# Two 256 x 256 transposes per graph moved from TensorE to VectorE, in 32 x 32 blocks

## The chip, the cores and the metric

The kernel runs on one core of a Trainium2 chip. A core has five engines that work side by side, each with a queue of instructions that it executes in order: TensorE (PE in the profile: matrix products; PEld its weight loads), VectorE (DVE), ScalarE (ACT), GpSimd (POOL) and SyncE (SP, which only issues transfers here). Sixteen DMA engines move data between the chip's memory (HBM) and the on-chip buffers (SBUF). Engines wait for each other by semaphores. The metric is the device time of one execution in microseconds, the median of several runs.

## The reference

64 graphs of 256 nodes with 256 features go through two layers; each layer adds its result to its input and normalises over the features.

```python
# layer 0
deg = adj.sum(-1);  d = deg ** -0.5                    # deg 0 counts as 1
x1 = layernorm(x + (d[:, :, None] * adj * d[:, None, :] + alpha * I) @ x @ W.T + b)
# layer 1, on x1; xc is x1 transposed to (features, nodes)
h = relu(bn1(conv1(xc)))                               # 1 tap
x_conv = relu(bn2(conv2(h)) + xc).T                    # 17 taps along the nodes
s = x1 @ w_se.T + b_se                                 # 3 coordinates per node
A = exp(-squared_distance(s, s)) * adj
x_nmp = A @ relu(x1 @ w_msg.T + b_msg)
r, z, n = gates([x_conv, x_nmp], x1)                   # a GRU cell
out = layernorm(x1 + (1 - z) * n + z * x1)
```

Inputs and weights are float32. Everything is computed in float32.

## The kernel before

A matmul on TensorE sums over the partition axis of both operands, so what is to be summed must lie on the partitions. Two operands lie the wrong way round: adj, whose transpose `adjT` (256 x 256, two halves of 128 partitions) feeds layer 0's product and the mask of the distances, and `x1`, the output of layer 0, whose transpose fills the first half of the tile `xn` and feeds conv1 and the messages. Both are transposed on TensorE today.

**Stages.** The graphs go in four groups of 16. Conv2 with its 17 taps is done in the frequency domain: the node axis is cut in pieces of 32, DFT'd (`p_dft`, L469), multiplied per frequency with the transformed weights (`p_k`, L526, over a whole group) and turned back; VectorE does the turning. So each group has three kinds of work: the front of its 16 graphs (layer 0 and layer 1 up to the message passing), the products, and the gates of its graphs (`p_rz` L804, `p_n` L841). Beside the front of the first 13 graphs, the transformed conv2 weights are made: taps are loaded (L276 to L278, SP), scaled (L285, DVE), transformed (`p_u`, L293, eight matmuls), copied out of TensorE's banks (L296, ACT, four copies into `u_set`), combined (difference L298 on DVE, sum L299 on POOL) and stored (L301). In the second group a few graphs' fronts run among the products and the others alone; in the later groups they run among the products or beside the gates of the group before.

**Layer 0 of a graph** (`layer0`, L337), in three pieces. The first: degrees by ScalarE with an accumulated sum (L347), `dis` = deg to the power −1/2 on POOL (L360), four transposes of 128 x 128 on TensorE into the bank `p_adjT` (L369) and one ScalarE copy into `adjT` (L370), the scaled diagonal on DVE (L372), x scaled by `dis` into the tile `x1` (L382, ACT; noted as `X_SCALED`), and x + b (L383, POOL). The second: `p_hT` (L390) and its copy (L395). The third: `p_out` (L400), scaled and added to x by DVE into `x1` (L405), the layer norm of `x1` in place (statistics on DVE L311 to L313, the power on POOL L314, L322 on DVE, the last step on ACT L324), and a store of `x1` to `x1_d` in HBM (L410, on ScalarE's DMA queue), which the gates read later.

**Layer 1 of a graph** (`layer1`, L422), in seven pieces: x1 transposed if it isn't yet (L419, copy L420); conv1 (`p_conv` L434, added bias L437 on DVE, relu L438 on ACT); messages (`p_msg` L455, L458, L459); the DFT (L469, copies L474); the coordinates as rows (L482 to L486); the distances (L493), exp (L494) and the product with `adjT` (L495); the message passing (`p_nmp` L502, copied to the second half of `xn` at L506, stored at L507). Where the graph is in the set `ALONE`, the transposes of x1 of the next graph are issued just before `p_nmp` (L498).

**What sets the order.** The program is a set of generators. `graphs` (L917) runs layer 1 of graph g; between its pieces it puts the pieces of layer 0 of graph g+2 and "other" work, by the table

```python
PLACES = (("other",), ("layer0",), (), (), ("layer0",), ("other", "layer0"), ())
```

A framework schedules what the generators issue, tracks the tiles, inserts the waits, and leaves a fixed order for each engine. A tile of a pool with `bufs=n` rotates over n buffers; who writes it waits for the last reader of the buffer's old contents. `adj_t`, `x_t`, `x1` and `xn` have two buffers, `h`, `hT` and `msg` one. `load(g)` (L95) issues adj and x of graph g whole, 256 KB each, on SP's queue.

The output of conv2 is transposed too (`transposed`, L765, bank `p_xcT` L772, with relu on ScalarE), which the change leaves as it is.

Of the kernel before, what the change touches and what calls it, by code (L numbers as in the profile page):

```python
# [9 lines left out]
F32 = mybir.dt.float32  # L10
# [4 lines left out]
P = 128  # L15
# [11 lines left out]
def kernel(  # L27
# [27 lines left out]
    nc = tc.nc  # L55
    B, N, D = x.shape
# [3 lines left out]
    NCH = N // P  # L60
    DCH = D // P


    FL, NT = 48, 32
    GT = N // NT
    Q = P // GT
    NQ = B // Q
    assert N == 256 and D == 256 and B % Q == 0 and TAPS == FL - NT + 1 and FL == 3 * NT // 2
# [6 lines left out]
    loads = ctx.enter_context(tc.tile_pool(name="loads", bufs=2))  # L75
# [4 lines left out]
    def bank(name):  # L80
        return ps.tile([P, 512], F32, tag="bank", name=name)
# [10 lines left out]

    xin, ain = {}, {}

    def load(g):  # L95
        if g >= B:
            return
        ain[g] = loads.tile([P, NCH, N], F32, name="adj_t")
        nc.sync.dma_start(ain[g], adj[g].rearrange("(c p) m -> p c m", p=P))
        xin[g] = loads.tile([P, NCH, D], F32, name="x_t")  # L100
        nc.sync.dma_start(xin[g], x[g].rearrange("(c p) f -> p c f", p=P))

# [9 lines left out]
    vectors = const.tile([16, P], F32, name="bn_in")  # L112
    neg_half = const.tile([P, 4], F32)
    nc.vector.memset(neg_half, -0.5)
    load(0)
    nc.scalar.dma_start(alpha_t, bcast_rows(alpha, 1))

    nc.scalar.copy(bc1[:, :4], neg_half)
    for i, a in enumerate((bn1_g, bn2_g, bn1_b, bn2_b, bn1_m, bn2_m, bn1_v, bn2_v)):
        (nc.sync if i % 2 else nc.scalar).dma_start(vectors[2 * i : 2 * i + 2], a.rearrange("(c p) -> c p", p=P))  # L120
    nc.scalar.dma_start(w0, w0T.rearrange("(k p) o -> p k o", p=P))
    load(1)
    nc.sync.dma_start(b0_t, bcast_rows(b0, D))
    nc.sync.dma_start(wc1[:, :, :D], conv1T.rearrange("(k p) o -> p k o", p=P))
    nc.sync.dma_start(wc1[:, :, D:], w_seT.rearrange("(k p) o -> p k o", p=P))
# [204 lines left out]
    x1_d = [dram.tile([Q, N, D], F32, name=f"x1_d{q}") for q in range(NQ)]  # L330
    xn_d = [dram.tile([P, 2 * DCH, N], F32, name=f"xn_d{g}") for g in range(B)]
    XN = {}
    ALONE = set()
    ADJT, X1, X_SCALED, DIAGONAL = {}, {}, {}, {}


    def layer0(g):  # L337

        a_t, x_t = ain.pop(g), xin.pop(g)

        adjT = work.tile([P, NCH, 3, P], F32, name="adjT", bufs=3)
        ADJT[g] = adjT

        deg = small.tile([P, NCH], F32, name="deg")
        def degrees():
            for c in range(NCH):
                nc.scalar.activation(  # L347
                    adjT[:, c, 0:2, :].rearrange("p n q -> p (n q)"), a_t[:, c, :], AF.Copy,
                    accum_out=deg[:, c : c + 1],
                )  # L350

        if g == 1:

            with tc.issue_after(X_SCALED[0]):
                degrees()
        else:
            degrees()
        nc.vector.scalar_tensor_tensor(deg, deg, 0.0, deg, op0=ALU.is_equal, op1=ALU.add)  # L358
        dis = small.tile([P, NCH], F32, name="dis")
        nc.gpsimd.tensor_tensor(dis, deg, neg_half[:, :NCH], op=ALU.pow)  # L360
        adeg = small.tile([P, NCH], F32, name="adeg")
        nc.vector.tensor_scalar(adeg, deg, alpha_t, None, op0=ALU.mult)

        p = bank("p_adjT").rearrange("p (c n) -> p c n", c=NCH)
        for mc in range(NCH):
            for c in range(NCH):
                nc.tensor.transpose(p[:, mc, c * P : (c + 1) * P], a_t[:, c, mc * P : (mc + 1) * P], ident)  # L369
        copied = nc.scalar.copy(adjT[:, :, 0:3:2, :], p.rearrange("p c (n q) -> p c n q", q=P))  # L370
        for mc in range(NCH):
            DIAGONAL[g] = nc.vector.scalar_tensor_tensor(  # L372
                adjT[:, mc, 1, :], ident, adeg[:, mc : mc + 1], adjT[:, mc, 2 * mc, :],
                op0=ALU.mult, op1=ALU.add,
            ).ins


        x1 = work.tile([P, NCH, D], F32, name="x1")
        X1[g] = x1
        with tc.issue_after(copied.ins) if g < 2 else ExitStack():  # L380
            for c in range(NCH):
                X_SCALED[g] = nc.scalar.activation(x1[:, c, :], x_t[:, c, :], AF.Copy, scale=dis[:, c : c + 1]).ins  # L382
        nc.gpsimd.tensor_tensor(x_t, x_t, b0_t.unsqueeze(1).to_broadcast([P, NCH, D]), op=ALU.add)  # L383

        yield
        hT = work.tile([P, DCH, N], F32, name="hT", bufs=1)
        p = bank("p_hT").rearrange("p (k n) -> p k n", k=DCH)
        for k in range(DCH):
            for mc in range(NCH):
                nc.tensor.matmul(  # L390
                    p[:, k, :], x1[:, mc, k * P : (k + 1) * P],
                    adjT[:, mc, 1 - mc : 3 - mc, :].rearrange("p n q -> p (n q)"),
                    start=mc == 0, stop=mc == NCH - 1,
                )
        nc.scalar.copy(hT, p)  # L395
        yield
        p = bank("p_out0").rearrange("p (c o) -> p c o", c=NCH)
        for c in range(NCH):
            for k in range(DCH):
                nc.tensor.matmul(  # L400
                    p[:, c, :], hT[:, k, c * P : (c + 1) * P], w0[:, k, :], start=k == 0, stop=k == DCH - 1
                )
        for c in range(NCH):
            mark(
                nc.vector.scalar_tensor_tensor(  # L405
                    x1[:, c, :], p[:, c, :], dis[:, c : c + 1], x_t[:, c, :], op0=ALU.mult, op1=ALU.add
                )
            )
        layernorm(x1, nc.scalar)
        nc.scalar.dma_start(x1_d[g // Q][g % Q].rearrange("(c p) d -> p c d", p=P), x1)  # L410
        yield

    def x1_transposed(g):
        x1 = X1.pop(g)
        xn = XN[g] = work.tile([P, 2 * DCH, N], F32, name="xn")
        p = bank("p_x1T").rearrange("p (k n) -> p k n", k=DCH)
        for k in range(DCH):
            for c in range(NCH):
                nc.tensor.transpose(p[:, k, c * P : (c + 1) * P], x1[:, c, k * P : (k + 1) * P], ident)  # L419
        nc.scalar.copy(xn[:, :DCH], p)  # L420

    def layer1(g, V, place):  # L422
# [34 lines left out]
                )  # L457
        mark(nc.vector.tensor_tensor(msg, p, bmsg_t.unsqueeze(1).to_broadcast([P, NCH, D]), op=ALU.add))  # L458
        nc.scalar.activation(msg, msg, AF.Relu)  # L459
        yield  # L460


# [31 lines left out]
            nc.scalar.activation(aT[:, c].rearrange("p n q -> p (n q)"), p, AF.Exp, bias=nsq[:, c : c + 1], scale=2.0)  # L494
        mark(nc.vector.tensor_mul(aT, aT, adjT[:, :, 0:3:2, :]))  # L495
        yield
        if g in ALONE:
            x1_transposed(g + 1)  # L498
        p = bank("p_nmp").rearrange("p (k n) -> p k n", k=DCH)
        for k in range(DCH):  # L500
# [416 lines left out]
    def graphs(first, part, V, others):  # L917


        for i in part:  # L920
            load(first + i + 3)
            given = {"layer0": layer0(first + i + 2) if first + i + 2 < B else iter(()), "other": others[i]}
            for piece, _ in enumerate(layer1(first + i, V, i)):
                yield
                for name in PLACES[piece]:
                    if next(given[name], "end") != "end":
                        yield
            yield from given["other"]

    with tc.tile_pool(name="setup", bufs=1) as setup:  # L930
# [2 lines left out]
        nc.sync.dma_start(bmsg_t, bcast_rows(b_msg, D))  # L933
        firsts = merge(layer0(0), layer0(1))
        run(take(firsts, 2))
        load(2)
        tables(setup)
        run(firsts)
        scale2 = next(batch_norms(setup))
# [65 lines left out]
    for q in range(NQ):  # L1005
        first = (q + 1) * Q
        more = q + 1 < NQ
        end = complex_end(q)
        if more:
            if q:  # L1010
                others = [take(late, 3 if i % 3 == 0 else 2) for i in range(AHEAD)]
            else:
                others = [nothing() for _ in range(AHEAD)]
                ALONE.update(range(first, first + AHEAD))
            begin = graphs(first, range(AHEAD), V2, others)
        sums(0)
        real = real_transform()
        for step in range(STEPS):
            if step < 4:
                run(products(step))  # L1020
            else:
                run(merge(products(step), take(real, 1)))
                run(complex_begin(step))
            if q:
                run(take(late, (0, 1, 1, 1, 1, 1, 2, 1, 2, 1, 2, 1)[step] if more else step % 2))
            else:
                run(take(begin, 3))
        run(real)
        if not q:
            run(paced(begin, end, RATES[q]))  # L1030
        elif more:
            run(paced(chain(merge(take(late, 20), take(begin, 6), 3), begin), end, RATES[q]))
        else:
            run(paced(late, end, RATES[q]))
            run(end)
        if more:
            run(late)
            run(end)
            for f in range(0, FL, 12):
                nc.scalar.copy(V[:, f : f + 12, :, : AHEAD * GT], V2[:, f : f + 12])  # L1040
            if q == 0:
                scope.close()
                gate = ctx.enter_context(tc.tile_pool(name="gate", bufs=2))
            early = gates(q, range(EARLY))
            others = [take(early, 5 if q == 0 else 2) for _ in range(Q)]
            run(graphs(first, range(AHEAD, Q), V, others))
            run(early)
            if q == 0:
                scope, AHEAD, V2 = open_ahead(6)
                ctx.enter_context(scope)  # L1050
            late = gates(q, range(EARLY, Q))
        else:
            run(gates(q, range(Q)))
# [53 lines left out]
```

## Time and profile before

| | before |
|---|---|
| time, median of 3 runs | 2166.91 us (2165.66 to 2167.95) |
| span of the profiled execution | 2165.1 us |
| TensorE clock granted | 0.99 to 1.00 of full speed |
| DMA | 305.65 MB in 251,182 packets, mean 141 GB/s |
| L370, copy of `p_adjT` by ScalarE | 64 of 576 ns, 36.9 us busy |
| L495, product with `adjT` by VectorE | 64 of 692 ns, 44.3 us busy |
| chain that ended last | TensorE has 20% of the span, POOL 3%, VectorE 2% |

The page of a profile first gives the busy time of each engine with its share of the span, then the span in 40 equal slices, where each digit is the busy share of a slice in tenths (9 is 90% or more); for the DMA row it is the mean over the 16 engines. In the table of groups, a row is one line of the program on one engine: output <- inputs, partitions x elements, the count, then busy microseconds and mean nanoseconds of one, then the idle time of the engine just ahead of them and what ended it. In the timeline, a row is start in microseconds, length, engine, line, operation, tiles, count and, in brackets, the idle time before it. Engines are pipelined: the distance between the starts of neighbours says what an instruction costs, its length how long it is in flight.

### The profile page before, as it was taken

Reading aid. Unit: us, or ns where it says so; the run is one execution under the profiler, and the core shown is the slowest. Engines: PE = TensorE matmul, PEld = TensorE weight load, DVE = VectorE, ACT = ScalarE, POOL = GpSimd, SP = SyncE. Lnnn points to the kernel's source line nnn. Section 1 sums busy time; section 2 is a strip of 40 time slices with the busy share of each in tenths; the row PEclk is TensorE's granted clock in tenths of the full one; section 3 lists DMA queues with packets and bytes.
Section 4 is the critical chain, followed back from the end, with each engine's and each line's share of the span. In section 5 each row is a group of like instructions: output and inputs, shape, how many; then the busy total and the mean of one; then the engine's idle time right before and its main releaser. Section 6 shows DMA issues by size and latency. Waiting matters only on the chain. (4 is left out here: it accounts for less than half of the span.)

```text
span 2165.1 us, 29037 instructions
## 1 busy us (share of the span) xinstructions
PE 2063.7 (95%) x9805; PEld 1749.6 (81%) x9805; DVE 1546.6 (71%) x3691; ACT 833.8 (39%) x1847; POOL 665.5 (31%) x640
## 2 busy tenths in 40 slices
PE   7999999888999999999999999899999998999998
PEld 5788788776778887788888888778888887888887
DVE  5555568775568798865556989775556889977776
ACT  4565643456331133455443122446443112222222
POOL 2444310122431243323222133323231124444442
PEclk9999999999999999999999999999999999999999
DMA  4765656435346644343336654334334844444441
GB/s 125 224 198 183 212 185 208 148 132 154 90 132 214 201 116 122 97 132 112 106 95 189 203 162 122 113 103 137 97 98 132 246 114 122 126 122 103 113 106 55
DMA packets 251182, 305.65 MB, mean 141 GB/s; under 512 B 18174, under 2 KB 229714, under 8 KB 251034
## 3 DMA queue, kind: packets, MB, share of 16 engines
q1 hardware_dynamic: 183530, 200.46, 30.1%
q10 hardware_dynamic: 44480, 67.39, 8.8%
q0 software_dynamic: 23024, 35.95, 8.6%
q8 instruction: 78, 1.28, 0.2%
q14 instruction: 70, 0.57, 0.1%
HBM read 200.62 MB, written 103.06 MB: 140 GB/s over the span
## 5 line engine op out<-in xcount | busy, mean ns | idle before, releaser
L841 PE MATMUL p_n<-wn,inputs 128*128 128x256 f32 x1536 | 357.6, 387 | 9.9 <-DVE first L817 9.4
L804 PE MATMUL p_rz<-wrz,sums 128*128 128x256 f32 x1536 | 348.8, 380 | 3.9 <-POOL sums L783 3.1
L841 PEld LDWEIGHTS p_n<-wn,inputs 128*128 128x128 f32 x1536 | 290.4, 193 | 57.3 <-DVE first L817 13.1
L804 PEld LDWEIGHTS p_rz<-wrz,sums 128*128 128x128 f32 x1536 | 289.7, 190 | 47.8 <-issue 5.2
L804 PE MATMUL p_rz<-wrz,inputs 128*128 128x256 f32 x1152 | 271.6, 379 | 0.0
L314 POOL TENSOR_TENSOR ln_rs<-ln_rs,neg_half 128x2 f32<-128x2 f32 x129 | 101.2, 784 | 521.4 <-DVE ln_rs L313 410.2
L804 PEld LDWEIGHTS p_rz<-wrz,inputs 128*128 128x128 f32 x1152 | 217.5, 190 | 29.7 <-ACT inputs L774 0.4
L853 ACT ACTIVATE nn<-gn 128x256 f32<-128x256 f32 x128 | 53.2, 416 | 333.1 <-DVE gn L850 333.0
L526 PE MATMUL p_k<-u,VM 128*128 128x256 f32 x736 | 174.3, 380 | 0.3 <-DMA u<-ud 0.3
L360 POOL TENSOR_TENSOR dis<-deg,neg_half 128x2 f32<-128x2 f32 x64 | 46.6, 727 | 408.9 <-DVE deg L358 405.5
L783 POOL TENSOR_TENSOR sums<-inputs 128x384 f32<-128x384 f32 x64 | 67.8, 1059 | 332.9 <-ACT inputs L774 326.2
L324 ACT ACTIVATE x_g<-x_g,ln_mr,ln_rs 128x256 f32<-128x256 f32 x128 | 70.0, 593 | 245.3 <-DVE ln_mr L322 245.3
L526 PEld LDWEIGHTS p_k<-u,VM 128*128 128x128 f32 x736 | 138.5, 190 | 20.8 <-DMA u<-ud 1.2
L469 PE MATMUL p_dft<-fwd,h 128*128 128x240 f32 x512 | 120.2, 379 | 20.7 <-ACT h L438 19.7
L390 PE MATMUL p_hT<-adjT,x 128*128 128x256 f32 x512 | 126.7, 390 | 12.8 <-DVE adjT L372 7.7
L434 PE MATMUL p_conv<-wc,xn 128*128 128x259 f32 x512 | 126.2, 388 | 6.8 <-ACT xn L420 5.6
L383 POOL TENSOR_TENSOR x_t<-x_t,b_t 128x512 f32<-128x512 f32 x64 | 87.6, 1370 | 138.9 <-ACT x L382 88.1
L469 PEld LDWEIGHTS p_dft<-fwd,h 128*128 128x128 f32 x512 | 95.8, 192 | 41.2 <-ACT h L438 34.5
L495 DVE TENSOR_TENSOR aT<-aT,adjT 128x512 f32<-128x512 f32 x64 | 44.3, 692 | 114.6 <-ACT aT L494 114.6
L400 PE MATMUL p_out<-w,hT 128*128 128x256 f32 x512 | 124.4, 386 | 1.5 <-ACT hT L395 0.9
L455 PE MATMUL p_msg<-wmsg,xn 128*128 128x256 f32 x512 | 121.3, 380 | 0.0
L502 PE MATMUL p_nmp<-aT,msg 128*128 128x256 f32 x512 | 121.1, 379 | 0.2 <-DVE aT L495 0.2
(154 smaller groups left out, 3897.9 us busy)
## 6 DMA issues: line engine op xcount, KB each, us to landing
u<-ud SPq DMA_DIRECT2D x284, 256.0 KB
xn_d<-xn ACTq DMA_DIRECT2D x64, 512.0 KB
inputs<-xn_d SPq DMA_DIRECT2D x64, 512.0 KB
ud<-u_set POOLq DMA_DIRECT2D x39, 480.0 KB, 6.1
adj_t<-in_adj_dram SPq DMA_DIRECT2D x64, 256.0 KB
x_t<-in_x_dram SPq DMA_DIRECT2D x64, 256.0 KB
x_d<-x ACTq DMA_DIRECT2D x64, 256.0 KB
xc_d<-VM SPq DMA_DIRECT2D x64, 256.0 KB
```

Of the source, the lines that this page charges most:

```text
L314: nc.gpsimd.tensor_tensor(rs[:, : len(chunks)], rs[:, : len(chunks)], neg_half[:, : len(chunks)], op=ALU.pow)
L324: nc.scalar.activation(y[:, c, :], y[:, c, :], AF.Identity, bias=mr[:, c : c + 1], scale=rs[:, c : c + 1])
L383: nc.gpsimd.tensor_tensor(x_t, x_t, b0_t.unsqueeze(1).to_broadcast([P, NCH, D]), op=ALU.add)
L390: nc.tensor.matmul(p[:, k, :], x1[:, mc, k * P : (k + 1) * P], adjT[:, mc, 1 - mc : 3 - mc, :].rearrange("p n q -> p (n q)"), start=mc == ...
L400: nc.tensor.matmul(p[:, c, :], hT[:, k, c * P : (c + 1) * P], w0[:, k, :], start=k == 0, stop=k == DCH - 1)
L434: nc.tensor.matmul(p, x1T[:, k, c * P : (c + 1) * P], wc1[:, k, :], start=k == 0, stop=k == DCH - 1)
L455: nc.tensor.matmul(p[:, c, :], x1T[:, k, c * P : (c + 1) * P], wmsg[:, k, :], start=k == 0, stop=k == DCH - 1)
L469: nc.tensor.matmul(p[:, t0 * FL : t1 * FL], h[:, c, k * P : (k + 1) * P], fwd[:, first : first + t1 - t0, :].rearrange("p t f -> p (t f)") ...
L502: nc.tensor.matmul(p[:, k, :], msg[:, mc, k * P : (k + 1) * P], aT[:, mc].rearrange("p n q -> p (n q)"), start=mc == 0, stop=mc == NCH - 1,)
L526: nc.tensor.matmul(p[:, j * D : (j + 1) * D], v[:, k, :], u[:, k, :], start=k == 0, stop=k == DCH - 1)
L804: nc.tensor.matmul(p[:, j * D : (j + 1) * D], a[:, k], wrz[:, b, k], start=k == 0, stop=k == HALF - 1)
L841: nc.tensor.matmul(p[:, o * D : (o + 1) * D], lhsT, w, start=j == 0, stop=j == len(part) - 1)
```

## The change

adj (graphs 2 to 63) and x1 (graphs 1 to 63) are transposed by VectorE. Its transpose works inside 32 x 32 blocks: each block is transposed in its place, the blocks themselves aren't exchanged. So the load exchanges them: block (i, j) is fetched to where block (j, i) was. `fetch_blocks` does it with four transfers for one matrix, each to 32 partitions, with 16 runs of 32 elements (128 bytes) a partition. adj is therefore loaded twice, once as it is for the degrees and once by blocks, in the same two rotating buffers; x1 is read back from its store in HBM, during layer 1 of the graph before it. The tile `x1` then needs to live only until its store is through and gets one buffer instead of two, which makes room for the blocks of x1. The transposes of x1 of the next graph are now issued ahead of `p_nmp` for every graph. The load of adj moves behind layer 0's first piece. The purpose is to take transposes and copies off TensorE and ScalarE.

```diff
+    def fetch_blocks(blocks, y):
+        for b in range(NB):
+            nc.sync.dma_start(
+                blocks[b * RB : (b + 1) * RB], y.rearrange("(s r) (k b j) -> b r k s j", r=RB, k=DCH, j=RB)[b]
+            )
...
+        a_t, a_b = loads.tile([P, NCH, N], F32, name="adj_t", tag="adj"), None
+        nc.sync.dma_start(a_t, adj[g].rearrange("(c p) m -> p c m", p=P))
+        if g > 1:
+            a_b = loads.tile([P, DCH, N // RB, RB], F32, name="adj_blocks", tag="adj")
+            fetch_blocks(a_b, adj[g])
...
-        p = bank("p_adjT").rearrange("p (c n) -> p c n", c=NCH)
-        for mc in range(NCH):
-            for c in range(NCH):
-                nc.tensor.transpose(p[:, mc, c * P : (c + 1) * P], a_t[:, c, mc * P : (mc + 1) * P], ident)
-        copied = nc.scalar.copy(adjT[:, :, 0:3:2, :], p.rearrange("p c (n q) -> p c n q", q=P))
+        if a_b is None:
...
+        else:
+            nc.vector.transpose(
+                adjT[:, :, 0:3:2, :].rearrange("p k n (s r) -> p k n s r", r=RB),
+                a_b.rearrange("p k (n s) j -> p k n s j", n=NCH),
+            )
...
-        x1 = work.tile([P, NCH, D], F32, name="x1")
+        x1 = work.tile([P, NCH, D], F32, name="x1", bufs=1, tag="x1" if g else "x1_blocks")
...
+    def fetched(g):
+        XB[g] = work.tile([P, DCH, N // RB, RB], F32, name="x1_blocks", bufs=1)
+        fetch_blocks(XB[g], x1_d[g // Q][g % Q])
...
         xn = XN[g] = work.tile([P, 2 * DCH, N], F32, name="xn")
+        if g:
+            nc.vector.transpose(xn[:, :DCH].rearrange("p k (s r) -> p k s r", r=RB), XB.pop(g))
+            return
...
         nc.scalar.activation(msg, msg, AF.Relu)
+        if g + 1 < B:
+            fetched(g + 1)
         yield
...
-        if g in ALONE:
+        if g + 1 < B:
             x1_transposed(g + 1)
...
-            load(first + i + 3)
+            load_x(first + i + 3)
...
                     if next(given[name], "end") != "end":
+                        if name == "layer0" and piece == 1:
+                            load_adj(first + i + 3)
                         yield
...
-                ALONE.update(range(first, first + AHEAD))
```

More of the change, by code (lines that the diff above doesn't have):

```diff
@@ L65 @@
     GT = N // NT
+    RB = 32
+    NB = P // RB
     Q = P // GT
@@ L93, with load_adj, load_x @@
     xin, ain = {}, {}
-    def load(g):
+    def fetch_blocks(blocks, y):
[3 more added lines that the diff above has]
+            )
+    def load_adj(g):
         if g >= B:
             return
-        ain[g] = loads.tile([P, NCH, N], F32, name="adj_t")
-        nc.sync.dma_start(ain[g], adj[g].rearrange("(c p) m -> p c m", p=P))
+        a_t, a_b = loads.tile([P, NCH, N], F32, name="adj_t", tag="adj"), None
[3 more added lines that the diff above has]
+            fetch_blocks(a_b, adj[g])
+        ain[g] = a_t, a_b
+    def load_x(g):
+        if g >= B:
+            return
         xin[g] = loads.tile([P, NCH, D], F32, name="x_t")
@@ L114 @@
     nc.vector.memset(neg_half, -0.5)
-    load(0)
+    load_adj(0)
+    load_x(0)
     nc.scalar.dma_start(alpha_t, bcast_rows(alpha, 1))
@@ L121 @@
     nc.scalar.dma_start(w0, w0T.rearrange("(k p) o -> p k o", p=P))
-    load(1)
+    load_adj(1)
+    load_x(1)
     nc.sync.dma_start(b0_t, bcast_rows(b0, D))
@@ L332 @@
     XN = {}
-    ALONE = set()
+    XB = {}
     ADJT, X1, X_SCALED, DIAGONAL = {}, {}, {}, {}
     def layer0(g):
-        a_t, x_t = ain.pop(g), xin.pop(g)
+        a_t, a_b, x_t = *ain.pop(g), xin.pop(g)
         adjT = work.tile([P, NCH, 3, P], F32, name="adjT", bufs=3)
@@ L362, in layer0 @@
         nc.vector.tensor_scalar(adeg, deg, alpha_t, None, op0=ALU.mult)
-        p = bank("p_adjT").rearrange("p (c n) -> p c n", c=NCH)
-        for mc in range(NCH):
-            for c in range(NCH):
-                nc.tensor.transpose(p[:, mc, c * P : (c + 1) * P], a_t[:, c, mc * P : (mc + 1) * P], ident)
-        copied = nc.scalar.copy(adjT[:, :, 0:3:2, :], p.rearrange("p c (n q) -> p c n q", q=P))
+        if a_b is None:
+            p = bank("p_adjT").rearrange("p (c n) -> p c n", c=NCH)
+            for mc in range(NCH):
+                for c in range(NCH):
+                    nc.tensor.transpose(p[:, mc, c * P : (c + 1) * P], a_t[:, c, mc * P : (mc + 1) * P], ident)
+            copied = nc.scalar.copy(adjT[:, :, 0:3:2, :], p.rearrange("p c (n q) -> p c n q", q=P))
+        else:
[3 more added lines that the diff above has]
+            )
         for mc in range(NCH):
@@ L415, in x1_transposed @@
         xn = XN[g] = work.tile([P, 2 * DCH, N], F32, name="xn")
+        if g:
+            nc.vector.transpose(xn[:, :DCH].rearrange("p k (s r) -> p k s r", r=RB), XB.pop(g))
+            return
         p = bank("p_x1T").rearrange("p (k n) -> p k n", k=DCH)
@@ L935 @@
         run(take(firsts, 2))
-        load(2)
+        load_adj(2)
+        load_x(2)
         tables(setup)
```

## The prediction

> **What bounds the kernel now.** I read the busy shares first, then the slices, the costliest groups, and last the timeline of single graphs.
>
> ```profile
> PE 2063.7 (95%) x9805; PEld 1749.6 (81%) x9805; DVE 1546.6 (71%) x3691; ACT 833.8 (39%) x1847; POOL 665.5 (31%) x640
> ...
> PE   7999999888999999999999999899999998999998
> ...
> DVE  5555568775568798865556989775556889977776
> ...
> DMA  4765656435346644343336654334334844444441
> ```
>
> TensorE (PE) is busy 95% of the span, and from slice 2 on in every slice; the trace's own ends of matmuls are modelled, so the weight loads' 81% are the firmer figure. VectorE (DVE) has 29% free on average, but the digits 8 and 9 of its row show stretches that are nearly full. So whatever leaves TensorE is time won, as long as TensorE waits for nothing new. The change touches these groups, kept apart by shape:
>
> ```profile
> L369 PE MATMUL p_adjT<-ident,adj_t 128*128 128x128 f32 x256 | 39.8, 279 | 7.1 <-DMA adj_t<-in_adj_dram 7.1
> ...
> L419 PE MATMUL p_x1T<-ident,x 128*128 128x128 f32 x256 | 39.1, 275 | 0.0
> L420 ACT COPY xn<-p_x1T 128x512 f32<-128x512 f32 x64 | 37.6, 587 | 6.1 <-PE p_x1T L419 5.8
> ```
>
> After the first bar stand busy time and the mean ns of one, after the second the idle time before them. The transposes overlap in the pipeline, so 275 ns isn't what one costs. The timeline of one graph of the first stage (start, length) tells:
>
> ```profile
> 163.84 1.23 DVE L298 TENSOR_TENSOR u_set<-u_set,u_set 120x1024 f32<-120x1024 f32 x1
> ...
> 165.10 0.88 DVE L405 SCALAR_TENSOR_TENSOR x<-p_out,dis,x_t 128x256 f32<-128x256 f32 x2
> ...
> 166.02 0.60 PE L419 MATMUL p_x1T<-ident,x 128*128 128x128 f32 x4
> ...
> 166.45 1.89 PE L293 MATMUL p_u<-taps,dft_w 85*120 85x256 f32 x8
> ...
> 168.18 1.92 PE L434 MATMUL p_conv<-wc,xn 128*128 128x259 f32 x8
> ...
> 169.68 1.09 ACT L324 ACTIVATE x<-x,ln_mr,ln_rs 128x256 f32<-128x256 f32 x2 [2.39 <-DVE ln_mr L322]
> ```
>
> From L419's start to that of the next matmuls is 0.43 us; 169.94 to 170.37 gives the same for L369's four. L469 starts at 156.34 and again at 172.37, so a graph takes 16.03 us here. To be noted for later: conv1 (L434) starts 2.16 us after the x1 transposes, and waits for no part of the layer norm of the next graph (L324), which comes after it.
>
> **What the skill says.** The Trainium skill, "VectorE: DVE Perf Modes", The three transpose paths, gives VectorE's 32x32 blocks 311 ns for 128x128 bf16, inside blocks only, hence the exchanged blocks in the load. No DVE transpose is in this trace. "TensorE: Matmul & The Clock Gate", Part 4, has about 275 ns for a PE transpose in a kernel: the trace agrees with 275 to 279 ns as a duration, but shows a pitch of 0.11. "DMA: Bandwidth & Descriptors", Why small descriptors are slow, states a fixed cost per packet; in this trace 1 KB packets take some 57 ns (queue 1: 30.1% of 16 x 2165.1 us over 183,530 packets).
>
> **The change part by part.**
>
> *Leaves TensorE and ScalarE.* adj of graphs 2 to 63 (62 sets) and x1 of graphs 1 to 63 (63 sets): 125 sets of four transposes x 0.435 = **−54.4 us** of PE, if nothing new is waited for. The 125 ScalarE copies of 0.58 us (73 us) go too; ScalarE is at 39%, so I count nothing for them alone.
>
> *Comes to VectorE.* 125 transposes of 128x512 f32. The nearest row of that shape is the product at L495, 692 ns; twice that data moves in L298's 1.23 us, my upper bound for a transpose that makes two passes; the lower is 0.31 (the skill's price, for a quarter of the data and half its bytes). I take 0.7: 125 x 0.7 = 88 us, which takes the mean from 71% to 75%. Not a bound by itself; its place in the queue is.
>
> *Comes to the DMA queues.* Each fetch is four transfers of 512 pieces of 128 bytes, so 4096 packets a graph for both matrices. Tiny packets (12-byte rows at 10.8 us) show 9.5 ns each as recorded and 36 ns by rate over 16 engines; 57 ns is the upper end. So 2.4, 9.2 or 14.6 us of all 16 engines a graph. The first stage uses about 0.65 x 16.0 = 10.4 us a graph already (the windows there show shares of 0.56 to 0.76), so 12.8, 19.6 or 25.0. I take 10 to 36 ns, which fits in the period worked out next.
>
> *New waits: x1 through HBM.* x1 is stored after the layer norm and read back in blocks during the next graph's layer 1, so that trip has most of a period. A store of this size (256 KB out, 1596.18, to the load that waits for it, 1598.47) lands 2.3 us after issue. But the x1 tile has one buffer instead of two: the next graph's scaling of x (L382), which today follows the layer norm at once, waits until the store has landed, and in ScalarE's order the relu of h (L438) and so the DFT stand behind it.
>
> *New place in VectorE's order.* This is what decides for me. In before, the x1 transposes are TensorE's, gated by nothing. In the changed program, VectorE's instructions of a first-stage graph run: layer-norm statistics, their product with the mean (L322's, waiting for POOL's power), adj's transpose, diagonal, u_set's difference (L298's), x1's transpose, conv1's additions. The difference waits for the ScalarE copies of all four p_u banks, three of them behind the layer norm's two activations. So conv1 of graph g+1 now waits, by queue order alone, for the layer norm of graph g+2, four copies, a difference and a transpose. Set p_out's start (L400) to 0, with TensorE's order p_out, p_nmp, p_u x8, p_conv, p_msg, p_dft, p_rows, p_hT, p_dist. The matmuls ahead of conv are through at 7.0. The layer norm starts on ScalarE at 6.6 (7.1 today: 162.56 to 169.68), ends at 7.65; the copies still due take it to 9.7; the difference 1.23 to 11.0; the transpose 0.7 to 11.7; conv starts at 11.8. From conv to the next p_out is 1.76 + 1.70 + 1.73 + 0.22 + 1.82 + 0.63 = 7.9 by today's pitches: period 19.6 to 19.7 against 16.04, or +3.6 in spite of the 0.87 won. Twelve graphs: **+43 us**.
>
> *Graphs 13 to 15*, without p_u: conv behind the x1 transpose, relu behind scaling: some 15.4 for 13.5, three graphs, **+6**.
>
> *Second group.* Three graphs run among products: −0.87 each, **−3**. Nine run alone (14.16 us a graph, from 442.06 to 456.22) with x1's transpose behind the layer norm and the turning operations in the same queue: five by my schedule 16.6 (+2.5), four, where adj's transpose and VM's operations also stand ahead, 19.2 (+5): **+32**.
>
> *The 24 graphs beside the gates*: the gates' matmuls stand between p_nmp and the store's landing, nothing is waited for: −0.87 x 24 = **−21**. *Twelve among the later products*: **−10**.
>
> Sum: +43 + 6 − 3 + 32 − 21 − 10 = +47, so 2167 + 47 = **2214**.
>
> **The rivals.** *TensorE's gain comes through.* 2167 − 54 = 2113; with a third to half of the layer-norm wait left, up to 2150. For it: TensorE is the bound, VectorE has room, and its queue holds gate matmuls or products in half of the stages. Against: the two orders above, in which nothing is left for TensorE between p_u and conv. *The DMA queues become the bound.* At 57 ns a packet the first stage takes 25.1 against 19.6 (+5.5 x 12 = 66), and the stretches with a share of 0.35 to 0.45 today (some 6 us of 14 a graph) need 6 + 14.6 = 21 for a 16 to 19 of mine: about +25 on the lone graphs and +55 on those beside the gates, in all about 2360. For it: the DMA digits of 6 and 7 in the first slices; against: no engine time in the tiny packets' record comes near 57. *Loss and gain cancel*: if the scaling and the transposes are only half as late as scheduled, +81 becomes +40 and the sum is +40 − 34 = +6, some 2155 to 2180.
>
> **How the numbers follow.** Mine, 2180 to 2255: 0.53. Gain comes through, 2113 to 2155: 0.25. DMA bound, 2255 to 2360: 0.14. Cancelled, 2155 to 2180: 0.08. Faster takes the second and a part of the last, 0.28; same 0.04; slower 0.68. The range leaves out the best third of the gain case and the upper half of the DMA case, some 0.17: 2128 to 2290. The transpose's bounds (0.31 to 1.23 us) move my sum by −10 to +15 and lie inside.
>
> **What would show it.** In the changed kernel's first stage: weight loads of conv1 idle some 4 us a graph, released by VectorE's x1 transpose; that transpose behind the u_set difference; 19 to 20 us from one p_dft to the next. In the groups: a DVE transpose near 0.7 us. The scaling of x idle some 2 us, released by the x1 store. Beside the gates: periods shorter by 0.9 us and PE without idle time. DMA share in the first stage under 0.95. I am wrong if conv1 starts without a wait there (then 2113 to 2150), if the transpose takes over 1.3 us (then VectorE's full stretches bind), or if the blocks' transfers are what x1's transpose waits for.

## The result, and the profile after

| | before | after |
|---|---|---|
| time, median | 2166.55 us (2165.66 to 2167.95, 4 runs) | 2252.59 us (2246.07 to 2254.43, 4 runs) |
| ratio to before | | 1.039 (1.0378 to 1.0404) |
| VectorE transposes of 128x512 | none | 125, of 701 and 709 ns |
| packets on DMA queue 1 | 183,530, 30.1% of 16 engines | 447,530, 38.3% |

The changed kernel is 86 us slower, where 47 were forecast. Its page, first the busy shares, then the slices of TensorE, VectorE, its clock and the DMA engines:

```profile
PE 2053.0 (91%) x9305; PEld 1728.4 (77%) x9305; DVE 1600.6 (71%) x3816; ACT 779.4 (35%) x1722; POOL 668.0 (30%) x640
...
PE   6777878977799999989899999989899999999998
...
DVE  5444455876756888887466788887565889987776
...
PEclk8899989998999999999999999999999999999999
DMA  5666667764464764445555764455553754444432
```

The loss is where TensorE's digits fell, mostly from 9 or 8 to 8 or 7: in all but one of the first eleven of 40 slices. TensorE's granted clock falls there too, which it didn't in the kernel before. VectorE's busy share stays at 71%, and no digit of its row is above the highest of before. The waits of the weight loads (waiting line, what it waited for, microseconds, times, the longest) point to the cause; the x1 transpose is L450 now, conv1 L470:

```profile
PEld p_conv L470 <- DVE xn L450: 90.7, 25, 6.5
PEld p_dft L507 <- ACT h L474: 22.5, 21, 3.1
PEld p_conv L470 <- DVE deg L379: 20.4, 4, 8.0
```

One graph of the first stage, from the timeline of the changed kernel, in the form in which the prediction showed one:

```profile
173.69 1.99 PE L428 MATMUL p_out<-w,hT 128*128 128x256 f32 x8
...
179.74 0.71 DVE L394 STREAM_TRANSPOSE adjT<-adj_blocks 128x512 f32<-128x512 f32 x1
179.76 1.09 ACT L345 ACTIVATE x<-x,ln_mr,ln_rs 128x256 f32<-128x256 f32 x2 [1.73 <-DVE ln_mr L343]
...
181.29 1.56 ACT L317 COPY u_set<-p_u 120x512 f32<-120x512 f32 x3
...
182.89 1.23 DVE L319 TENSOR_TENSOR u_set<-u_set,u_set 120x1024 f32<-120x1024 f32 x1 [1.78 <-ACT u_set L317]
...
184.03 0.70 DVE L450 STREAM_TRANSPOSE xn<-x_blocks 128x512 f32<-128x512 f32 x1
...
184.79 3.42 PE L470 MATMUL p_conv<-wc,xn 128*128 128x259 f32 x8 [3.92 <-DVE xn L450]
...
194.18 1.99 PE L428 MATMUL p_out<-w,hT 128*128 128x256 f32 x8
```

The chain is the one that was forecast: layer norm of the next graph, copies, u_set difference, x1's transpose, conv1. It puts conv1 11.1 us after p_out. The transposes themselves hardly ever wait for their blocks. In the groups of the whole execution, with the idle time after the second bar:

```profile
L450 DVE STREAM_TRANSPOSE xn<-x_blocks 128x512 f32<-128x512 f32 x63 | 44.1, 701 | 2.4 <-DMA x_blocks<-x_d 2.4
L394 DVE STREAM_TRANSPOSE adjT<-adj_blocks 128x512 f32<-128x512 f32 x62 | 43.9, 709 | 0.9
```

From 125 to 285 us, in the first stage, no VectorE instruction waits for a transfer.

What was not forecast is in conv1's own length: 3.42 us for the eight matmuls that took 1.92 before. The granted clock over the stretches of this graph (window, its length, busy PE, PEld, DVE, ACT, POOL with counts, clock, DMA share, GB/s) shows why:

```profile
177.25:180.87 3.62, 3.62 (x17) 2.74 (x15) 2.43 (x12) 1.70 (x4) 1.38 (x2) 1.00 0.62 216
180.87:184.79 3.92, 0.00 (x1) 0.00 (x1) 2.08 (x3) 2.89 (x6) 2.42 (x2) 0.93 0.66 187
184.79:188.05 3.26, 3.26 (x9) 2.63 (x10) 0.43 (x1) 0.00 (x0) 3.26 (x4) 0.56 0.51 144
188.05:194.18 6.13, 6.09 (x32) 4.84 (x30) 2.12 (x7) 2.87 (x7) 0.50 (x1) 1.00 0.99 251
```

After 3.92 us without a matmul TensorE runs the next 3.26 us at 0.56 of its clock. So a long wait is paid once as idle time and once more, about 1.5 us here, as slow matmuls.

Where along the program the time goes is read from the store of xn, once a graph (L507 before, L545 after, on ScalarE's queue): its time after minus its time before. The forecast for each part is summed from the prediction's own terms: of its second group, graph 16 falls in the second row and graphs 28 to 31, which run beside the gates, in the third.

| graphs | difference at the end of the part | this part | forecast |
|---|---|---|---|
| 1 to 12 (beside the taps) | 53.9 us | +53.9 | +43 |
| 13 to 16 | 61.8 | +7.9 | +5 |
| 17 to 31 (second group) | 97.0 | +35.2 | +27 |
| 32 to 63 | 86.1 | −10.9 | −28 |

### The profile page after: what moved, and what is told of

It is laid out like the page before. It is cut to its first block, busy times and chain, and to the rows that moved or that the text cites. A ratio compares the mean times of both kernels' runs of the same rounds, so it can differ in the third digit from the quotient of the medians.

```text
span 2252.7 us, 28769 instructions
## 1 busy us (share of the span) xinstructions
PE 2053.0 (91%) x9305; PEld 1728.4 (77%) x9305; DVE 1600.6 (71%) x3816; ACT 779.4 (35%) x1722; POOL 668.0 (30%) x640
## 3 DMA queue, kind: packets, MB, share of 16 engines
q1 hardware_dynamic: 447530, 233.26, 38.3%
## 5 line engine op out<-in xcount | busy, mean ns | idle before, releaser
L470 PE MATMUL p_conv<-wc,xn 128*128 128x259 f32 x512 | 158.7, 463 | 100.0 <-DVE xn L450 79.8
L470 PEld LDWEIGHTS p_conv<-wc,xn 128*128 128x128 f32 x512 | 115.7, 233 | 133.1 <-DVE xn L450 90.7
L411 POOL TENSOR_TENSOR x_t<-x_t,b_t 128x512 f32<-128x512 f32 x64 | 84.7, 1324 | 205.3 <-ACT x L410 101.7
L507 PE MATMUL p_dft<-fwd,h 128*128 128x240 f32 x512 | 119.7, 378 | 14.2 <-ACT h L474 13.9
```

Source lines behind the costliest of these rows:

```text
L470: nc.tensor.matmul(p, x1T[:, k, c * P : (c + 1) * P], wc1[:, k, :], start=k == 0, stop=k == DCH - 1)
L507: nc.tensor.matmul(p[:, t0 * FL : t1 * FL], h[:, c, k * P : (k + 1) * P], fwd[:, first : first + t1 - t0, :].rearrange("p t f -> p (t f)") ...
```

## The experiments

**Each half alone.** The first keeps adj's part and puts x1 back on TensorE with two buffers; the second keeps x1's part and puts adj back.

```diff
# adj alone
-        if g:
-            nc.vector.transpose(xn[:, :DCH]..., XB.pop(g))
-            return
...
-        x1 = work.tile(..., name="x1", bufs=1, tag="x1" if g else "x1_blocks")
+        x1 = work.tile(..., name="x1")
# x1 alone
-        if g > 1:
+        if g > B:
             a_b = loads.tile(...)
```

> Only adj is transposed by VectorE (62 graphs, fetched in blocks); x1 goes back to TensorE with its two buffers, issued as in the kernel before. Queue-place theory (the loss is x1's transpose standing in VectorE's queue behind the next graph's layer norm): conv1 waits for nothing new, TensorE wins 62 x 0.435 = 27 us, 2140 (2132 to 2152), period of the first stage about 15.6. Transfer theory (the 128-byte packets cost the time): half of the packets are still there, so about half of the 86 us, 2190 or more. Buffer theory (x1's single buffer makes the scaling wait for the store): as the first, 2140.

> Only x1 is transposed by VectorE (63 graphs, read back in blocks, one buffer); adj stays on TensorE. Queue-place theory: in the order that was built, x1's transpose stands behind the layer norm's statistics but ahead of the u_set difference in the first stage, so conv1 waits well under 1 us there and the period is 16.0 to 17.3; the second group's lone graphs keep their loss of some 40 us, and adj's 27 us aren't won: 2205 to 2240. Transfer theory: half of the packets, 2205 to 2215, with the first stage sharing the loss evenly. Buffer theory: all of the loss stays, and the first stage's period stays over 19.

adj alone takes 2243.44 us (ratio 1.036, 1.0342 to 1.0373), a clear miss for the queue-place theory as I had put it. x1 alone takes 2230.97 (1.030, 1.028 to 1.0311). Its total is within what was expected, and conv1 no longer waits for x1's transpose from graph 2 to 12; but the first stage takes 17.9 us a graph, over the 16.0 to 17.3 expected: there p_u now waits 1.2 us a graph for the scaled taps and p_hT 0.5 for the addition to the messages, both VectorE's. The losses are not halves of one: alone, adj's part loses 77 us and x1's 65 of the 86, in other places. adj alone takes 23.2 to 25.5 us a graph in the first stage and loses nothing more in the rest. Its timeline there:

```profile
218.87 0.70 DVE L394 STREAM_TRANSPOSE adjT<-adj_blocks 128x512 f32<-128x512 f32 x1
...
220.31 1.23 DVE L319 TENSOR_TENSOR u_set<-u_set,u_set 120x1024 f32<-120x1024 f32 x1 [0.75 <-ACT u_set L317]
220.36 3.38 POOL L320 TENSOR_TENSOR u_set<-u_set,u_set 120x1024 f32<-120x1024 f32 x1 [1.45 <-ACT u_set L317]
221.46 2.69 DVE L399 SCALAR_TENSOR_TENSOR adjT<-ident,adeg,adjT 128x128 f32<-128x128 f32 x2
...
224.03 3.75 PE L418 MATMUL p_hT<-adjT,x 128*128 128x256 f32 x8 [4.37 <-DVE adjT L399]
```

Now p_hT waits for 4.37 us, for the diagonal that follows adj's transpose, and that diagonal stands behind the same u_set difference. With the instructions for one graph moved, the scheduler laid VectorE's queue out anew and the wait came out at another operand. So the theory fits in a wider form only, found after the result: it isn't x1's transpose, it is that an operand of TensorE now comes from VectorE's one queue, behind work that itself waits. Two more things make the graph longer. p_hT's eight matmuls take 3.75 us after the wait, for 1.89 before. And the two diagonals take 2.69 us where they take 0.61 elsewhere, while GpSimd works on its sum.

**x1's transpose put first.** Its blocks are fetched one piece earlier, and it is ordered ahead of the next graph's addition of x to p_out, which precedes the layer norm on VectorE.

```diff
+        if g + 1 < B:
+            x1_transposed(g + 1)          # ahead of layer 0's third piece
         yield
...
+        with tc.issue_after(X1T[g - 1]) if g > 1 else ExitStack():
             for c in range(NCH):
                 mark(nc.vector.scalar_tensor_tensor(x1[:, c, :], p[:, c, :], ...))
```

> All as changed, but x1's blocks are fetched one piece earlier (during conv1 instead of after the messages), and x1's transpose is put ahead of the next graph's first layer-norm instruction on VectorE in all 62 cases. Queue-place theory: conv1's wait goes, the first stage takes 15.2 to 16.3 a graph, the lone graphs of the second group 13.5 to 15, and the time is 2112 to 2150. Transfer theory: same packets, 2225 or more, with x1's transpose waiting for its blocks. Buffer theory: relu still stands behind the scaling, which waits for the store: first stage 17.5 to 19, 2180 to 2220.

2288.20 us (1.056, 1.0547 to 1.0579): a miss, and slower than the changed kernel. conv1's waits did fall, from 90.7 to 13.2 us. Another took their place:

```profile
PEld p_hT L418 <- ACT x L410: 107.2, 29, 6.9
PEld p_dft L508 <- ACT h L475: 44.9, 28, 3.6
...
PEld p_conv L471 <- DVE xn L451: 13.2, 16, 3.3
```

and in its timeline:

```profile
205.70 0.37 ACTq L439 DMA_DIRECT2D x_d<-x  x1
...
211.09 0.91 ACT L410 ACTIVATE x<-x_t,dis 128x256 f32<-128x256 f32 x2 [3.87 <-DMA x_d<-x]
...
211.65 3.61 PE L418 MATMUL p_hT<-adjT,x 128*128 128x256 f32 x8 [6.53 <-ACT x L410]
```

The scaling of x waits for the store of x1, because x1 has one buffer: 5.4 us from issue to the scaling, where the prediction took 2.3 for the landing and the changed kernel needs 2.4 (180.88 to 183.28). In the changed kernel this wait is hidden behind conv1's. Here VectorE's layer norm comes later, so the store does too, and p_hT stands behind it. The later store also has company: between 205.7 and 211.1 the packets of GpSimd's queue, which stores the transformed weights, take 43.5% of the 16 engines and those of ScalarE's queue, which stores x1, 14.7%; in the changed kernel, from 180.88 to 183.3, GpSimd's queue moves nothing. That the company makes the store slow is a reading of these shares, not a test.

**Two buffers for x1**, first alone, then together with x1's transpose put first.

```diff
-        x1 = work.tile([P, NCH, D], F32, name="x1", bufs=1, tag="x1" if g else "x1_blocks")
+        x1 = work.tile([P, NCH, D], F32, name="x1")
...
-    ustream = ctx.enter_context(tc.tile_pool(name="ustream", bufs=6))
+    ustream = ctx.enter_context(tc.tile_pool(name="ustream", bufs=5))
```

> All as changed, but the tile x1 has two buffers again; the room for it is taken from the stream of transformed conv2 weights (five buffers instead of six). Queue-place theory: the scaling isn't what ends last ahead of conv1, so the first stage stays at 20 to 20.5 a graph and the time within 12 us of the changed kernel, 2240 to 2260. Buffer theory: the waits of the scaling for the store (65 us in the changed kernel) go and most of the loss with them, 2190 or less. Transfer theory: 2245 to 2255.

> The run with x1's transpose ahead of the layer norm, and two buffers for x1 on top (weight stream of five buffers instead of six). There the wait had moved to the scaling of x behind the store of x1 (107 us of p_hT's waits). If queue place and single buffer together are what x1's part costs: p_hT's waits for the scaling fall under 25 us, the lone graphs of the second group (20 to 30) lose no more than 8 us against the kernel before instead of 18 to 25, the first stage takes 16.5 to 18 a graph, 2185 to 2215 in all. If VectorE and GpSimd hold each other up whatever the order, the first stage stays over 20 and the total over 2240.

Alone: 2314.27 us (1.068, 1.066 to 1.0696), the slowest of all, and another miss; the first stage takes 23.9 us a graph with VectorE's order there unchanged. Its timeline:

```profile
201.08 1.27 POOL L411 TENSOR_TENSOR x_t<-x_t,b_t 128x512 f32<-128x512 f32 x1
201.59 4.14 DVE L319 TENSOR_TENSOR u_set<-u_set,u_set 120x1024 f32<-120x1024 f32 x1 [2.17 <-ACT u_set L317]
202.30 2.34 POOL L320 TENSOR_TENSOR u_set<-u_set,u_set 120x1024 f32<-120x1024 f32 x1
...
205.66 0.70 DVE L450 STREAM_TRANSPOSE xn<-x_blocks 128x512 f32<-128x512 f32 x1
```

The scaling no longer waits, so GpSimd's x + b (L411), which needs it, comes some 3 us earlier in the graph. It is running when VectorE's difference begins, GpSimd's sum follows at once, and the difference ends only 1.1 us after both: 4.14 us for 1.23. Taking a wait away moved a neighbour into the critical instruction.

Together with the early transpose: 2229.66 (1.030, 1.0277 to 1.0322). p_hT's waits for the scaling fall from 107.2 to 20.5 us, as expected, and graphs 21 to 30 lose 9 us where the changed kernel loses 23 (8 or less was expected). The first stage takes 17.9 to 21.1, over the 16.5 to 18 forecast, and so does the total. Together, queue place and buffer are 14 of the 23 us in those graphs, but they don't account for the first stage: there p_hT now waits 1.9 us a graph for the diagonals on VectorE (13.0 us in seven graphs).

**GpSimd's sum left out** of the run with two buffers.

```diff
-                nc.gpsimd.tensor_tensor(us[2], us[0], us[1], op=ALU.add)
-                for d, u in zip(ud, (us[0], us[3], us[2])):
+                for d, u in zip(ud, (us[0], us[3], us[1])):
```

> The run with two x1 buffers, with GpSimd's sum of the u_set halves left out (the first half is stored in the sum's place, so conv2's transformed weights are not the right ones); VectorE's order in the first stage is unchanged. There VectorE's u_set difference took 4.14 us where it takes 1.23 elsewhere, while GpSimd worked. If GpSimd's work at the same time stretches it: 1.2 to 2.0 us here, with only x + b left on GpSimd, and the first stage takes 20 to 21.5 a graph instead of 23.9, some 30 to 45 us less in all (2270 to 2285). If the difference waits for something else (the copies, the store of the weights): 3.5 us or more, and the period stays above 23.

In the groups by shape of its first stage:

```profile
L319 DVE TENSOR_TENSOR u_set<-u_set,u_set 120x1024 f32<-120x1024 f32 x7 | 13.0, 1853 | 15.2 <-ACT u_set L317 15.2
```

1.85 us for 4.14: GpSimd's work at the same time is what stretched it, and 0.6 us more than 1.23 is left while x + b runs. The Trainium skill, "SBUF — State Buffer", SBUF: two separate sides, says that VectorE with two SBUF inputs and a GpSimd operation that reads SBUF lock each other out for a whole instruction; the two lengths agree: each time the difference ends 1.1 us after GpSimd's last overlapping operation. The period falls from 23.9 to 22.2 and the time to 2298.44, 16 us less instead of 30 to 45: with two buffers the scaling stands between the copies in ScalarE's queue, so the difference still begins late, and the eight matmuls after the wait are as slow as before (3.6 to 3.8 us).

**The difference behind x1's transpose**, the one link of the predicted chain that a single ordering edge removes.

```diff
+                with tc.issue_after(X1T[n]) if n else ExitStack():
                     nc.vector.tensor_sub(us[3], us[1], us[0])
```

> All as changed, but for the first 13 graphs VectorE's u_set difference is put behind x1's transpose of the same graph, so the transpose no longer waits for the four copies and the difference; adj's transpose and the layer norm still stand ahead of it. If the place in VectorE's queue makes the wait: conv1 starts some 3 us earlier than in the changed kernel (8 us after p_out instead of 11), the slow clock after the wait is shorter, the first stage takes 17 to 18.3 a graph, 2212 to 2230 in all. If the later graphs' waits or VectorE's meeting with GpSimd (which stretched the difference to 4.1 us in the run with two x1 buffers) set it: the difference runs against GpSimd's sum, takes 3 us or more, holds up conv1's additions, and the period stays at 20 or more.

2218.04 us (1.024, 1.0226 to 1.0263), 34 us less than the changed kernel, within the forecast. In its timeline:

```profile
163.21 0.70 DVE L451 STREAM_TRANSPOSE xn<-x_blocks 128x512 f32<-128x512 f32 x1
163.97 2.02 PE L471 MATMUL p_conv<-wc,xn 128*128 128x259 f32 x8 [0.91 <-DVE xn L451]
165.07 1.23 DVE L320 TENSOR_TENSOR u_set<-u_set,u_set 120x1024 f32<-120x1024 f32 x1 [1.16 <-ACT u_set L317]
```

In this graph conv1 waits 0.91 us instead of 3.92 and takes 2.02 us again, and the first stage takes 17.4 us a graph instead of 20.5. With the slow matmuls that follow from it, this link is 36 of the 54 us that graphs 1 to 12 had lost (17.6 here).

**Whole rows for blocks.** The same bytes into the same tiles in an eighth of the packets; block exchange is left out.

```diff
-                blocks[b * RB : (b + 1) * RB], y.rearrange("(s r) (k b j) -> b r k s j", ...)[b]
+                blocks[b * RB : (b + 1) * RB].rearrange("r k s j -> r k (s j)"),
+                y.rearrange("(c b r) m -> b r c m", c=NCH, b=NB)[b],
```

> All as changed, but the four transfers of a fetch bring whole rows of 1 KB instead of 128-byte pieces, to the same tiles: the blocks aren't exchanged, so what is transposed isn't the transpose; the bytes are the same, the packets an eighth. VectorE's order in the first stage comes out as in the run before this one (x1's transpose ahead of the u_set difference), so the two are to be compared. Queue-place theory: first stage within 0.5 us a graph of that run, total within 15 us. Transfer theory: the packets cost several us of the DMA engines a graph, so the first stage is 2 us or more shorter and the total 40 us or more lower.

2229.02 us (1.030, 1.0279 to 1.0318), 11 us more than the run before it and not 40 less. The two could not be compared graph by graph as planned: one diagonal came to stand behind x1's transpose here, into GpSimd's sum, and the diagonals take 1588 ns in the mean instead of 349 (19.6 to 23.6 us a graph, so the expected 0.5 us was missed too). So this run gives the transfer theory no support, but can't exclude it alone. What speaks against it in the first stage is that nothing on VectorE waits for a transfer there in the changed kernel, and that the run before it took most of that stage's loss away with every packet in place.

**TensorE kept busy** through conv1's wait, for graphs 1 to 12.

```diff
+            if c == 0 and 0 < g < 13:
+                with tc.issue_after(LAST_U[-1]):
+                    for _ in range(16):
+                        nc.tensor.matmul(p, wmsg[:, 0, :P], wc1[:, 0, :], start=True, stop=True)
```

> All as changed, but for graphs 1 to 12 sixteen more matmuls (wmsg by the conv1 weights, into conv1's bank, overwritten by conv1) run between p_u and conv1 while TensorE would wait; both halves of p_u are issued together. If the clock falls because TensorE idles (0.56 in the changed kernel's stretch after the wait, eight matmuls of conv1 in 3.4 us against 1.9): conv1 takes 1.8 to 2.1 at a clock of 0.95 or more, the first stage 18.8 to 19.8 a graph, 2232 to 2246 in all. If the clock falls for another reason, or is only how the records show a late start: conv1 stays at 3 us or more, and the time is 2250 or more.

2285.75 us (1.056, 1.054 to 1.0572). The windows of one graph, the filling and conv1:

```profile
200.69:207.68 6.99, 6.99 (x34) 6.08 (x33) 5.42 (x7) 2.10 (x6) 5.71 (x5) 1.00 0.83 242
207.68:209.43 1.75, 1.75 (x10) 1.51 (x8) 0.43 (x1) 0.00 (x0) 1.27 (x1) 1.00 0.94 310
```

conv1 after the filling is back at a clock of 1.00 and eight matmuls in 1.75 us (3.26 in the changed kernel). So it is the idle time that slows it. The forecast of the time was a miss: each of the sixteen is two passes on the engine, 7 us where 3.9 were to be filled, and p_u now waits 1.2 us a graph for the scaled taps. The first stage takes 23.3 us a graph.

**The change where it should gain.** First for graphs 32 to 63, then only for 42 to 47 and 58 to 63.

```diff
-        if g > 1:
+        if g in BLOCKS:                   # likewise at the fetch and at x1's transpose
             a_b = loads.tile(...)
...
+    BLOCKS = (*range(42, 48), *range(58, 64))      # first: range(32, 64)
```

Where the change is off, adj is again loaded at the start of the graph, and the tiles x1 of even and odd graphs lie in two places, as with two buffers.

> The change for graphs 32 to 63 alone (they run beside the gates or among the products); graphs 0 to 31 as in the kernel before, in the same order on every engine. Queue-place theory: there the gates' matmuls fill TensorE while VectorE's queue is behind, so the stretch from graph 31 on keeps what the changed kernel won in it (its distance to the kernel before fell from 97 to 86 us): 2155 (2148 to 2162), faster than both. If all of that gain was the backlog of the first 32 graphs being made up: 2166 or more.

> The change for graphs 42 to 47 and 58 to 63 alone, which run beside the gates and after the group's first residual loads; all others as in the kernel before. In the changed kernel two such graphs took 37.7 us against 40.4, some 1.4 each, while the loss of 4 us of waiting and more of slow clock came once a group, at graphs 38 to 40 and 54 to 56, where the load of conv2's output waits among the block fetches. If that load is why graphs 32 to 63 together won nothing: this keeps 10 to 16 us, 2151 to 2158. If the gain beside the gates is only made-up backlog: 2164 to 2168.

The first, at 2164.06 us (0.9988, 0.9979 to 0.9998), keeps under 3 of the 12 us expected. It wins 0.9 to 2.1 us a graph in graphs 41 to 47, and loses about 9 at graphs 38 to 40 and 6 at 54 and 55. At the first of these, where the gates of a group begin:

```profile
987.28 0.37 SPq L790 DMA_DIRECT2D xc_g<-xc_d  x1
...
987.47 0.34 ACTq L547 DMA_DIRECT2D xn_d<-xn  x1
...
988.10 3.89 SPq L102 DMA_DIRECT2D adj_blocks<-in_adj_dram  x4
...
993.44 1.23 POOL L801 DMA_DIRECT2D xc_g<-x_d  x1 [4.47 <-DMA xc_g<-xc_d]
994.23 1.46 POOL L823 TENSOR_TENSOR sums<-inputs 128x384 f32<-128x384 f32 x1
...
995.74 1.22 PE L844 MATMUL p_rz<-wrz,sums 128*128 128x256 f32 x2 [3.74 <-POOL sums L823]
```

The same transfers in the kernel before:

```profile
985.15 0.37 SPq L750 DMA_DIRECT2D xc_g<-xc_d  x1
...
986.03 0.34 ACTq L507 DMA_DIRECT2D xn_d<-xn  x1
...
988.34 1.23 POOL L761 DMA_DIRECT2D xc_g<-x_d  x1 [2.60 <-PE p_adjT L369]
```

The load of conv2's output takes 6.2 us from issue to the accumulating transfer that follows it, where it took 3.2. GpSimd stands in that wait, its sums come late, and the gates' matmuls wait for them. The block fetches, issued just after the load, are at most the end of the delay. From 988.5 to 990.5, when by the order of issue the load's packets are due on SyncE's queue, the store of xn on ScalarE's queue has 56.7% of the 16 engines and SyncE's queue 30.1%, and only 5 packets under 512 bytes move; in the next 2 us there are 1009. In the kernel before, the load ran ahead of that store: from 986.2 to 987.2 SyncE's queue has 79.3% and ScalarE's 2.0%. With whole rows the same pair still takes 5.5 us, again beside that store (67.7% to 31.6%, 1049 to 1051.5). So what these packets show is a load that the change has moved into a store of 512 KB; how much the block fetches add to it was not separated. Without the change at these graphs, the second version takes **2154.14 us** (0.994, 0.9927 to 0.9952), 12 us less than the kernel before and as forecast.

## Why the prediction was right

The chain that decides was right, link by link. The size was right only by the width of the range: the sum was 39 us short, and the measured time lies 2.4 us inside the upper end, which is luck.

By its own steps:

- *VectorE's transpose at 0.7 us*: 701 and 709 ns, right.
- *What leaves TensorE*: 125 sets of four. Where nothing new is waited for, two graphs take 37.7 us after and 40.4 before, 1.4 a graph and so more than the 0.87 counted; why it is more wasn't tested.
- *conv1 behind the layer norm, the copies and the difference*: right in order and size, 11.1 us after p_out for the 11.8 forecast. That the difference makes 36 us of it, slow matmuls included, was shown by taking that link out.
- *Period of 19.6*: 20.5. The term left out is the clock after a wait, 1.5 us a graph; conv1's start, 0.7 earlier than forecast, hid part of it. In the whole kernel conv1's matmuls are busy for 158.7 us where they were for 126.2, 32 us that no step of the prediction had. The Trainium skill, "TensorE: Matmul & The Clock Gate", Part 1, states it (half clock after an idle window of some 3.4 us, and about as long to recover); the trace agrees, with 0.56 for 3.26 us after 3.92 us of idle time. The prediction drew on this page for the transposes and didn't price its waits with it.
- *The single x1 buffer*: the wait is there (65 us of ScalarE in all), but 0.43 us in the graph shown, where 2 were named as the sign, and hidden behind conv1 as the schedule had it. That it would bind as soon as conv1's wait went, only the runs showed.
- *Graphs beside the gates and in the later products, −31*: the step that failed. Graphs 28 to 31 gave −5.4, where −3.5 were counted, but graphs 32 to 63 −10.9 where −28 were counted. In the twelve that the prediction put among the later products (32 to 37 and 48 to 53) next to nothing is won, −3.2 and +1.3; why, no run shows. At the head of the gates graphs 38 to 40 and 54 to 56 lose 2.9 and 4.4: there, as read in the run with graphs 32 to 63 alone, the load of conv2's output comes late, beside the store of xn. The prediction said of these graphs that nothing is waited for, and priced transfers only as a share of the engines, not by which of them meet.
- *The DMA engines as the bound*: no. The 264,000 added packets take 12.8 ns each ((38.3% x 2252.7 − 30.1% x 2165.1) x 16 / 264,000), near the lower end of the estimate; 256,000 of them are pieces of 128 bytes. The first stage's DMA share is 0.66 to 0.70 over a graph, under the 0.95 given as the sign. Within a graph it reaches 0.99 (188.05 to 194.18), where TensorE works without a gap.

By the table, the 39 us that the sum was short are 11 in graphs 1 to 12 (18 of slow clock, less 8 for conv1's earlier start), 11 in graphs 13 to 31 and 17 in graphs 32 to 63. What stays open is why the first stage keeps 17.4 us a graph with the difference out of the chain, and 17.9 to 21 with early transpose and two buffers, against the 15.2 that the gain alone would give. In the first of these TensorE's waits still come to 1.4 us a graph, 1.1 of them conv1's for x1's transpose; in the second 1.9 us are p_hT's for the diagonals. The rest wasn't separated.

## What to carry to other kernels

An operation that leaves a full engine for one with room brings its operand's place in the other's queue with it: list what stands ahead of it there and what that waits for, at every operand that the engine feeds, before counting the time saved. In this kernel a wait of TensorE of some 4 us cost the wait plus about 1.5 us of slow matmuls. A change that moves transfers can cost more than their share of the engines where two others come to meet (here read from the packets, not tested): look at which transfers run at the same time. A change that wins in one part of a program and loses in another can be made in that part alone: 12 of 64 graphs gave −12 us where all of them gave +86.

## What was not expected of the hardware

TensorE's clock at 0.56 for 3.3 us after 3.9 us without work, and at 0.50 for 3.6 us after 6.2 (555.05 to 558.67 in the changed kernel), on a single core. VectorE and GpSimd operations on SBUF that stretch each other: 1.23 to 4.14 us for a difference, 0.61 to 2.69 for two diagonals. The added packets, mostly of 128 bytes, at 12.8 ns in the records, against 57 in the mean for those of queue 1 before, which average 1.1 KB. A load and a store of 256 KB that took about twice as long with other transfers beside them: 6.2 for 3.2 us and 5.4 for 2.4.
